# Fused layer chain: a front with split loads and another embedding layout, and one grid operation placed ahead of each division of the attention

## The chip, the cores and the metric

The kernel runs on one core of a Trainium2 chip. Its time is the device time of one execution in microseconds, and the median of several executions is compared. Beside it there is one execution recorded by the hardware profiler, from which all durations below are read. Engines are named as in the profile: PE is TensorE (PEld its weight loads), DVE is VectorE, ACT is ScalarE, POOL is GpSimd, SP is SyncE, which here only issues transfers. A "q" behind an engine's name means its queue of issued transfers.

## The reference, cut to what matters

Eight samples of 512 x 512 float32 pass through four layers. The first two are touched by the change.

```python
# layer 0: one explicit time step of a grid equation, per sample f[b] (512 x 512)
Af, Bf = A_grid[None] * f[:, None], B_grid[None] * f[:, None]
df = -(grad(Af[:,0],1) + grad(Af[:,1],2)) \
     + 0.5 * (grad2(Bf[:,0],1) + grad2(Bf[:,1],2)
              + grad(grad(Bf[:,2],2),1) + grad(grad(Bf[:,2],1),2))
x = maximum(f + df * dt[:, None, None], 0)      # one-sided formulas at all four borders

# layer 1: attention block, 16 heads of 32, an additive bias per head, a mask per sample
emb = silu(sin_emb(timestep)) @ W_ada + b_ada    # (8, 1024)
scale, shift = split(emb)
x = layernorm(x) * (1 + scale) + shift
q, k, v = x @ Wq + bq, x @ Wk + bk, x @ Wv + bv
p = softmax(where(mask, -inf, q @ k.T / sqrt(32) + bias))
x = x + (p @ v) @ Wo + bo
x = x + gelu2(layernorm2(x) @ W1 + b1) @ W2 + b2
# layer 2: an MLP with the weights of one of 8 experts per sample (expert_idx), then a layernorm
# layer 3: a low-rank response scaled by a gate and by sigmoid(safety)
```

## The kernel before, in words

A sample is held as 128 partitions of 4 rows of 512 columns (`P`, `R`, `D`). There are three stages.

**The front, `grid_stage`.** It computes layer 0 for sample 0, whole. SP loads six planes of 1 MiB in this order: `b1`, `a1`, `b0`, `a0` (planes of `B_grid` and `A_grid`), `f` (sample 0) and `b2`. Then SP loads the two halves of `W_ada` (`wada`), the small rows `bqk`, `bvc`, `bo` (`load_rows`), and the four matrices `Wq`, `Wk`, `Wv`, `Wo` (`load_w`). ACT's queue carries a few small transfers. DVE makes the combined coefficient planes `ca`, `cb`, `cc`, `ce`, `cg`, multiplies each by `f`, and PE adds the shifted products into four PSUM tiles (`add`, through shifted identities `zi`). First and last rows of all eight samples are computed apart, on 64 partitions (`fe`, `ec`, up to `xe`), from "edge rows" that POOL's queue loads; a small POOL operation, `gate_e`, holds those loads until `b1` is there. A second gate, `gate_c`, lets go POOL's stores of the six coefficient planes to DRAM (`coef_q` ... `coef_b`, 1 MiB each), which samples 1 to 7 read back later. POOL's queue then stores the edge rows' results (`xed`), behind those planes. `embed`, `embed_turn` and `embed_out` compute the embedding: PE makes it with samples on partitions (two results of 8 x 512), ACT copies it, PE turns it, DVE adds `b_ada` in eight operations, into `sc1` and `shift`. Eight transfers put the edge rows of sample 0 into `x`. DVE then forms small constants for the borders, `gab` and `gte` ("ghosts"), the last part of them from `hg`, four tiny matmuls. Last, DVE and POOL normalise `x`.

The tiles of the next stage lie in memory that the front gives up, so the first transfer of the attention (`mu`, the mask) waits until the front's last readers and transfers are done, those of `xed` among them; the transposed `x1` tiles do so too.

**The attention, `attention_stage`.** 128 units (sample `b`, group of four heads `c`, row `r`), in an order written out by hand and kept by `pin`. In the loop over `i` the masks are added to the bias tiles of unit `i+1` (POOL, `add_mask`), the softmax of unit `i` runs (DVE, then ACT), the probabilities of unit `i-1` are turned (`turned`: PE into `tr`, two buffers, then copies `pt` by DVE and ACT in turn), and the products with v of unit `i-2` are formed (`values`). Every fourth unit `divide` ends a group: PE turns the reciprocal sums (`rb`), ACT copies them (`rbs`), DVE multiplies (`ct`). Behind that comes `inverse` (a reciprocal `rs` on DVE and a copy on ACT), then loads, and then `grid_step(i, grid_sums)`: DVE's share of layer 0 for the samples 1 to 7, spread over 16 units per sample by the table `GRID`. A letter of the table is one DVE operation over 128 x 1024 elements (`grid_op`), `n` is a normalisation on ACT, `s` its statistics. `grid_gate` is a small POOL operation that holds `add_mask` until the last such operation of the unit before has ended. `x1_in` turns the normalised sample (PE, `xtr`) and evicts it with scale and shift: groups 0 and 2 by ACT, 1 and 3 by DVE.

```python
            if pair and two[2] == R - 1:
                divide(two[0], two[1])
            if old:
                inverse(*old)
            ...
            grid_step(i, grid_sums)
            grid_step(i, grid_loads)
            if i + 1 < n:
                scores(*units[i + 1])
```

Once, in unit 2, `add_bv` runs: DVE spreads `bvc` into `bvr`, PE multiplies it by `Wo` (`pb`), and DVE adds that to `bo`.

**The rest, `mlp_stage`.** Both MLPs and the gated response, in passes of 256 rows.

## Time and profile before

| | us |
|---|---|
| median of 3 runs (lowest, highest) | 2859.53 (2859.52, 2860.22) |
| the profiled execution, its own time | 2864.53 |
| the profiled execution, its span | 2862.8 |
| granted TensorE clock, mean over the span | 0.986 |
| busy: PE, DVE, ACT, POOL | 2738.6, 1945.2, 1002.7, 1495.7 |
| first softmax operation of DVE starts at | 86.04 |
| last `ct` of the attention starts at | 1164.03 |
| moved by DMA over the span | 405.60 MB |

The profiled execution took 5.0 us longer than the median of the runs. A row of a timeline reads: start, duration, engine, line of the kernel, operation, result<-sources, shape, count, and in brackets how long the engine was idle before it and what released it. A row of stretches reads: the stretch and its length, busy time of PE, PEld, DVE, ACT and POOL with their instructions in brackets, granted clock, share of the DMA engines, GB/s.

### The profile page before, as it was taken

Reading aid. Unit: us, or ns where it says so; the run is one execution under the profiler, and the core shown is the slowest. Engines: PE = TensorE matmul, PEld = TensorE weight load, DVE = VectorE, ACT = ScalarE, POOL = GpSimd, SP = SyncE. Lnnn points to the kernel's source line nnn. Section 1 sums busy time; section 2 is a strip of 40 time slices with the busy share of each in tenths; the row PEclk is TensorE's granted clock in tenths of the full one; section 3 lists DMA queues with packets and bytes.
Section 4 is the critical chain, followed back from the end, with each engine's and each line's share of the span. In section 5 each row is a group of like instructions: output and inputs, shape, how many; then the busy total and the mean of one; then the engine's idle time right before and its main releaser. Section 6 shows DMA issues by size and latency. Waiting matters only on the chain.

```text
span 2862.8 us, 39706 instructions
## 1 busy us (share of the span) xinstructions
PE 2738.6 (96%) x14606; PEld 2008.5 (70%) x14606; DVE 1945.2 (68%) x3606; ACT 1002.7 (35%) x2133; POOL 1495.7 (52%) x1062
## 2 busy tenths in 40 slices
PE   5889999999999999999999999999999999999997
PEld 2455545454545555688888888887888888888885
DVE  7788888888888766576566656664456555656554
ACT  1366666666666666212111211211121121121221
POOL 2345455555555655366465555654545545545632
PEclk9999999999999999999999999999999999999998
DMA  8655656565666555433532444253133133143120
GB/s 306 210 192 178 218 170 230 167 229 171 224 203 207 162 159 184 165 100 81 154 122 61 127 138 123 49 166 112 59 110 126 52 141 125 49 144 111 41 74 30
DMA packets 190352, 405.60 MB, mean 142 GB/s; under 512 B 24321, under 2 KB 28993, under 8 KB 183631
## 3 DMA queue, kind: packets, MB, share of 16 engines
q1 hardware_dynamic: 185170, 391.94, 41.0%
q0 software_dynamic: 3680, 11.07, 3.1%
q8 instruction: 116, 1.90, 0.3%
q14 instruction: 78, 0.63, 0.1%
q10 hardware_dynamic: 1308, 0.07, 0.0%
HBM read 367.32 MB, written 31.50 MB: 139 GB/s over the span
## 4 chain that ended last, share of the span: by engine, by line
PE 79%; DVE 14%; ACT 4%; DMA 2%; issue 1%; POOL 0%; SPq 0%; ACTq 0%; DVEq 0%; POOLq 0%
PE u L1129 27%; PE y L1129 24%; PE tr L547 6%; PE ctx L544 4%; PE s L544 4%; PE o L544 3%; PE pv L544 3%; PE pq L544 2%; DVE x L664 2%; DVE bt L968 2%; ACT bt L973 2%; DVE pt L993 2%; PE pk L544 2%; DVE tb L1135 1%; DVE act L1135 1%
## 5 line engine op out<-in xcount | busy, mean ns | idle before, releaser
L1129 PE MATMUL y<-wo,act 128*128 128x256 f32 x2560 | 578.9, 381 | 0.0
L945 POOL TENSOR_TENSOR bt<-bt,mk 128x1024 f32<-128x1024 f32 x256 | 541.8, 2138 | 58.8 <-DMA bt<-in_bias 42.6
L1129 PEld LDWEIGHTS y<-wo,act 128*128 128x128 f32 x2560 | 479.4, 190 | 82.2 <-issue 20.5
L973 ACT ACTIVATE bt<-bt,mn 128x512 f32<-128x512 f32 x512 | 365.5, 715 | 137.0 <-DVE mn L968 136.7
L547 PEld LDWEIGHTS tr<-ident,bt 128*128 128x128 f32 x2048 | 229.1, 142 | 189.7 <-issue 118.6
L1129 PE MATMUL u<-bt,wi 128*128 128x256 f32 x1440 | 332.4, 381 | 0.0
L968 DVE CUSTOM_DVE_ANT_0 bt<-s,bt 128x512 f32<-128x512 f32 x512 | 330.5, 683 | 0.0
L547 PE MATMUL tr<-ident,bt 128*128 128x128 f32 x2048 | 282.7, 280 | 38.8 <-DVE pt L993 27.7
L1135 DVE TENSOR_TENSOR act<-u,u 128x512 f32<-128x512 f32 x256 | 173.4, 687 | 212.8 <-PE u L1129 138.0
L1129 PEld LDWEIGHTS u<-bt,wi 128*128 128x128 f32 x1440 | 274.6, 191 | 37.6
L993 DVE COPY pt<-tr 128x512 f32<-128x512 f32 x256 | 175.9, 687 | 100.4 <-PE tr L547 99.7
L1129 PE MATMUL u<-tb,ws 128*128 128x256 f32 x1024 | 242.4, 380 | 0.0
L1129 PE MATMUL y<-t,s 128*128 128x256 f32 x1024 | 234.1, 380 | 0.0
L1129 PEld LDWEIGHTS u<-tb,ws 128*128 128x128 f32 x1024 | 195.1, 191 | 26.7
L995 ACT COPY pt<-tr 128x512 f32<-128x512 f32 x256 | 148.2, 579 | 183.9 <-PE tr L547 181.5
L1138 POOL TENSOR_TENSOR t<-wo,t 128x512 f32<-128x512 f32 x64 | 104.5, 1648 | 198.2 <-PE y L1129 198.2
L1129 PEld LDWEIGHTS y<-t,s 128*128 128x128 f32 x1024 | 190.6, 190 | 23.8
L1135 DVE TENSOR_TENSOR x<-y,x 128x512 f32<-128x512 f32 x96 | 64.5, 686 | 183.2 <-PE y L1129 129.2
L1441 ACT ACTIVATE act<-act,bi 128x512 f32<-128x512 f32 x128 | 83.9, 712 | 292.3 <-DVE act L1135 292.2
L1441 ACT ACTIVATE act<-act,b 128x512 f32<-128x512 f32 x128 | 82.9, 712 | 292.4 <-DVE act L1135 292.4
L1135 DVE TENSOR_TENSOR u<-u,u 128x512 f32<-128x512 f32 x192 | 131.3, 684 | 59.5 <-PE u L1129 59.5
L544 PE MATMUL s<-kt,qt 32*128 32x512 f32 x1024 | 166.9, 644 | 2.1 <-DVE mn L968 1.1
(315 smaller groups left out, 4283.2 us busy)
## 6 DMA issues: line engine op xcount, KB each, us to landing
bt<-in_bias SPq DMA_DIRECT2D x256, 512.0 KB
wo<-in_W SPq DMA_DIRECT2D x32, 1024.0 KB
wi<-in_Wi SPq DMA_DIRECT2D x32, 1024.0 KB
wo<-in_Wo_e SPq DMA_DIRECT2D x32, 1024.0 KB
wi<-in_W SPq DMA_DIRECT2D x28, 1024.0 KB
gq<-coef_q SPq DMA_DIRECT2D x21, 512.0 KB
x1d<-x SPq DMA_DIRECT2D x8, 1024.0 KB
x<-x1d SPq DMA_DIRECT2D x8, 1024.0 KB
```

Source lines behind the costliest of these rows:

```text
L544: pin(nc.tensor.matmul(out, lhsT=lhsT, rhs=rhs, start=start, stop=stop))
L547: pin(nc.tensor.transpose(out, src, ident))
L664: pin(nc.vector.tensor_tensor(out, x, y, op))
L945: nc.gpsimd.tensor_tensor(bt, bt, mask[b, r][:, None, :].to_broadcast([P, 2, S]), ALU.add)
L968: nc.vector.tensor_tensor_reduce(bt[:, i, :], ss[h], bt[:, i, :], -1.0, 3.0e38, ALU.add, ALU.min, mn)
L973: nc.scalar.activation(bt[:, i, :], bt[:, i, :], AF.Exp, bias=mn, scale=-1.0, accum_out=sums[b, c, r][:, h : h + 1],)
L993: pin(nc.vector.tensor_copy(pt[:, :, r % 2, :], tr))
L995: pin(nc.scalar.copy(pt[:, :, r % 2, :], tr))
L1129: pin(nc.tensor.matmul(out, lhsT=lhsT, rhs=rhs, start=start, stop=stop))
L1135: pin(nc.vector.tensor_tensor(out, x, y, op))
L1138: pin(nc.gpsimd.tensor_tensor(out, x, y, op))
L1441: nc.scalar.activation(acts[g][:, k, :], acts[g][:, k, :], func, bias=bi[:, j : j + 1])
```

## The change

In words, front first:

- `b1` and `a1` are loaded in halves of two rows each, in turn, and `ca` and `cb` are formed half by half. The loads of `eidx` and `sigs` go from SP's queue to ACT's.
- `gate_e` reads `f` where it read `b1`: the edge rows are let go behind `f`. Their blocks come in another order, so that the results reach `x` by two transfers on each of SP's and ACT's queues, where it were four.
- `load_w` stands ahead of `load_rows`.
- The embedding is computed with features on partitions: 32 small matmuls with `wada` as the stationary operand, and one addition on DVE (`ada`, whose parts are `sc1` and `shift`); the 1 of `1 + scale` is added to `bada` beforehand. That addition stands behind the normalisation.
- The ghosts `gab` and `gte` are formed by POOL, behind the stores of the coefficient planes and ahead of `xed`. For that, `hg` is multiplied earlier and ACT copies it into `hgs`.
- At the start of the attention the loads of sample 1 (`gf`, `gq`) stand ahead of the first bias tiles. `bvr` is formed by ACT before the first unit.
- `x1_in` evicts groups 0 and 2 by DVE, 1 and 3 by ACT.
- In the units with a division, one operation of `GRID` (ahead of the bar) runs ahead of `divide`, the others where they were.

```diff
-    sc1 = const.tile([P, KC, NB], F32, name="sc1")
-    shift = const.tile([P, KC, NB], F32, name="shift")
+    ada = const.tile([P, 2 * KC, NB], F32, name="ada")
+    sc1, shift = ada[:, 0:KC, :], ada[:, KC : 2 * KC, :]
...
+    nc.scalar.dma_start(sigs, a["safety"][None, :].to_broadcast([P, NB]))
+    nc.scalar.dma_start(eidx, a["eidx"][None, :])
+    nc.vector.tensor_scalar(bada[:, 0:KC], bada[:, 0:KC], 1.0, None, ALU.add)
...
     def embed(ps):
+        pe = ps.tile([P, 2 * KC, NB], F32, name="pe")
         for m in range(2 * KC):
             o = (m % KC) * P
+            for k in range(KC):
+                tc.keep_in_program_order(
+                    nc.tensor.matmul(
+                        pe[:, m, :], lhsT=wada[m // KC][:, k, o : o + P], rhs=sc[:, k, :],
+                        start=k == 0, stop=k == KC - 1,
+                    )
+                )
         return pe
     def embed_out(pe):
+        tc.keep_in_program_order(
+            nc.vector.tensor_tensor(
+                ada, pe, bada[:, :, None].to_broadcast([P, 2 * KC, NB]), ALU.add
+            )
+        )
...
-        blocks = (0, 1, 3, 2)
+        blocks = (0, 2, 3, 1)
...
-            rows_in(b1, a["B"][1])
-            rows_in(a1, a["A"][1])
+            halves = slice(0, 2), slice(2, 4)
+            for h in halves:
+                rows_in(b1, a["B"][1], h)
+                rows_in(a1, a["A"][1], h)
...
             load_wada()
+            load_w()
             load_rows()
-            load_w()
...
-            pin(nc.gpsimd.tensor_tensor(gate, b1[:, 0, 0:1], b1[:, 0, 0:1], ALU.add))
+            pin(nc.gpsimd.tensor_tensor(gate, f[:, 0, 0:1], f[:, 0, 0:1], ALU.add))
...
-            tt(ca, b1, a1, ALU.add)
-            tt(cb, b1, a1, ALU.subtract)
+            for h in halves:
+                tt(ca[:, h, :], b1[:, h, :], a1[:, h, :], ALU.add)
+                tt(cb[:, h, :], b1[:, h, :], a1[:, h, :], ALU.subtract)
...
         add(lambda r: c[:, r, :])
+        hg = ps.tile([P, 2, 2, 3], F32, name="hg")
+        for i in range(2):
+            for k, (r, turn) in enumerate(((R - 1, 0), (0, 2))):
+                mm(
+                    hg[:, k, i, :], zi[:, 0, turn : turn + P],
+                    b2[:, r, 509 * i : 509 * i + 3], True, True,
+                )
+        hgs = small.tile([P, 2, 2, 3], F32, name="hgs", tag="hgs", bufs=1)
+        pin(nc.scalar.copy(hgs, hg))
...
+                pin(
+                    nc.gpsimd.tensor_tensor(
+                        tab if k else gab[:, :, i, :], c[:, :, o : o + 4], w, ALU.mult
+                    )
+                )
+            pin(nc.gpsimd.tensor_tensor(gab[:, :, i, :], gab[:, :, i, :], tab, ALU.add))
...
+                    pin(nc.gpsimd.tensor_scalar_mul(dst, src, w[k]))
         t = wp.tile([P, R, D], F32, name="t")
...
-        for i, k in enumerate(blocks):
-            c = slice(W * k, W * k + W)
-            pin(nc.sync.dma_start(x[0:1, 0, c], xe[n * i : n * i + 1, :]))
-            o = n * i + NB
-            pin(nc.scalar.dma_start(x[P - 1 : P, R - 1, c], xe[o : o + 1, :]))
+        for o, u, c in ((0, 3 * n, 0), (n, n, 2 * W)):
+            for side, q_ in ((0, nc.sync), (1, nc.scalar)):
+                p, r = side * (P - 1), side * (R - 1)
+                e0 = o + side * NB
+                pin(
+                    q_.dma_start(
+                        x[p : p + 1, r, c : c + 2 * W].rearrange("o (b w) -> o b w", w=W),
+                        xe[e0 : e0 + u + 1 : u, :],
+                    )
+                )
...
         stats(2)
-        embed_out(pe)
...
-                tt(tab if k else gab[:, :, i, :], c[:, :, o : o + 4], w, ALU.mult)
-            tt(gab[:, :, i, :], gab[:, :, i, :], tab, ALU.add)
...
-                    pin(nc.vector.tensor_scalar(dst, src, w[k], None, ALU.mult))
         stats(0)
...
+        embed_out(pe)
...
-            if c % 2 == 0:
+            if c % 2:
                 pin(nc.scalar.activation(tv, trv, AF.Identity, bias=h, scale=g))
...
         GRID = {
-            0: "q0 q1", 1: "e0", 2: "w0 c0 hh", 3: "C0", 4: "+0 -0", 5: "g0", 6: "G0 a0",
-            7: "A0 b0 B0", 8: "x0 q2", 9: "e1 w1 c1", 10: "C1 +1", 11: "-1 g1", 12: "G1 s0",
-            13: "n0 a1 A1 b1", 14: "B1 x1", 15: "s1", 16: "n1",
+            0: "q0 q1", 1: "e0 |", 2: "w0 c0 hh", 3: "C0", 4: "+0 -0", 5: "g0 |", 6: "G0 a0",
+            7: "A0 b0 B0", 8: "x0 q2", 9: "e1 | w1 c1", 10: "C1 +1", 11: "-1 g1", 12: "G1 s0",
+            13: "a1 | n0 A1 b1", 14: "B1 x1", 15: "s1", 16: "n1",
         }
...
         mask_in(0, 0)
+        grid_loads(1, -2)
         load_bias(*units[0])
-        grid_loads(1, -2)
         grid_loads(1, -1)
...
+        pin(nc.scalar.copy(bvr, bvc[:, :, None].to_broadcast([P, KC, P])))
...
-            if pair and two[2] == R - 1:
+            split = pair and two[2] == R - 1
+            if split:
+                grid_step(i, lambda n, j: grid_sums(n, j, late=False))
                 divide(two[0], two[1])
...
-            grid_step(i, grid_sums)
+            grid_step(i, lambda n, j: grid_sums(n, j, early=not split))
```

More of the change, by code (lines that the diff above doesn't have):

```diff
@@ L53, in fused_kernel @@
     nc.gpsimd.memset(phalf, 0.5)
-    sc1 = const.tile([P, KC, NB], F32, name="sc1")
-    shift = const.tile([P, KC, NB], F32, name="shift")
+    ada = const.tile([P, 2 * KC, NB], F32, name="ada")
+    sc1, shift = ada[:, 0:KC, :], ada[:, KC : 2 * KC, :]
     eidx = const.tile([1, NB], I32, name="eidx")
-    nc.sync.dma_start(eidx, a["eidx"][None, :])
     sigs = const.tile([P, NB], F32, name="sigs")
-    nc.sync.dma_start(sigs, a["safety"][None, :].to_broadcast([P, NB]))
-    nc.scalar.activation(sigs, sigs, AF.Sigmoid)
     def x_home(b):
@@ L138, in fused_kernel @@
     nc.scalar.activation(sc, sc, AF.Silu)
+    nc.scalar.activation(sigs, sigs, AF.Sigmoid)
     def embed(ps):
-        keep = tc.keep_in_program_order
-        out = []
-        for h in range(2):
-            pr = ps.tile([NB, D], F32, name=f"pe_{h}")
+        pe = ps.tile([P, 2 * KC, NB], F32, name="pe")
+        for m in range(2 * KC):
+            o = (m % KC) * P
             for k in range(KC):
-                keep(
+                tc.keep_in_program_order(
                     nc.tensor.matmul(
-                        pr, lhsT=sc[:, k, :], rhs=wada[h][:, k, :], start=k == 0, stop=k == KC - 1
-                    )
-                )
-            out.append(pr)
-        return out
-    def embed_turn(ps, rows, out):
-        for h in range(2):
-            tc.keep_in_program_order(nc.scalar.copy(rows[:, h, :], out[h]))
-        pe = ps.tile([P, 2 * KC, NB], F32, name="pe_t")
-        for m in range(2 * KC):
-            o = (m % KC) * P
-            tc.keep_in_program_order(
-                nc.tensor.transpose(pe[:, m, :], rows[:, m // KC, o : o + P], ident[0:NB, 0:NB])
-            )
+                        pe[:, m, :], lhsT=wada[m // KC][:, k, o : o + P], rhs=sc[:, k, :],
+                        start=k == 0, stop=k == KC - 1,
+                    )
+                )
         return pe
     def embed_out(pe):
-        for m in range(KC):
-            for t, o, one in ((sc1, m, 1.0), (shift, KC + m, 0.0)):
-                tc.keep_in_program_order(
-                    nc.vector.tensor_scalar(
-                        t[:, m, :], pe[:, o, :], bada[:, o : o + 1], one, ALU.add, ALU.add
-                    )
-                )
+        tc.keep_in_program_order(
[3 more added lines that the diff above has]
+        )
     dram = ctx.enter_context(tc.tile_pool(name="x1_dram", bufs=1, space=bass.MemoryType.DRAM))
@@ L194, in fused_kernel @@
         tc, a, const, small, dram, xt[0], mhalf, ident, load_wada, load_w, load_rows, embed,
-        embed_turn, embed_out,
+        embed_out,
     )
@@ L229, in grid_stage @@
     tc, a, const, small, dram, x, mhalf, ident, load_wada, load_w, load_rows, embed,
-    embed_turn, embed_out,
+    embed_out,
 ):
@@ L284, in grid_stage, with rows_in @@
         dte = gp.tile([N, 1], F32, name="dte")
-        def rows_in(t, src):
-            nc.sync.dma_start(t, src.rearrange("(p r) j -> p r j", r=R))
+        def rows_in(t, src, r=slice(0, R)):
+            nc.sync.dma_start(t[:, r, :], src.rearrange("(p r) j -> p r j", r=R)[:, r, :])
         with tc.tile_pool(name="raw", bufs=1) as rp:
@@ L393, in grid_stage @@
                 pin(nc.gpsimd.dma_start(coefs[m][S + 1 : S + 2, :], w[P - 1 : P, R - 1, :]))
+        gab = const.tile([P, R, 2, 4], F32, name="gab")
+        tab = small.tile([P, R, 4], F32, name="tab", tag="tab", bufs=1)
+        for i, (u, v, o) in enumerate(((ca, cb, 0), (cb, ca, 508))):
+            for k, c in enumerate((u, v)):
+                w = gw[:, None, 8 * i + 4 * k : 8 * i + 4 * k + 4].to_broadcast([P, R, 4])
+                pin(
[4 more added lines that the diff above has]
+            pin(nc.gpsimd.tensor_tensor(gab[:, :, i, :], gab[:, :, i, :], tab, ALU.add))
+        gte = const.tile([P, R + 2, 2, 3], F32, name="gte")
+        for i, (o, w) in enumerate(((0, (-3.0, 3.0, -1.0)), (509, (1.0, -3.0, 3.0)))):
+            for k in range(3):
+                for dst, src in (
+                    (gte[:, 1 : R + 1, i, k : k + 1], b2[:, :, o + k : o + k + 1]),
+                    (gte[:, 0 : R + 2 : R + 1, i, k : k + 1], hgs[:, :, i, k : k + 1]),
+                ):
+                    pin(nc.gpsimd.tensor_scalar_mul(dst, src, w[k]))
         t = wp.tile([P, R, D], F32, name="t")
@@ L397, in grid_stage @@
         add(lambda r: t[:, r, :], 1, last=True)
-        hg = ps.tile([P, 2, 2, 3], F32, name="hg")
-        for i in range(2):
-            for k, (r, turn) in enumerate(((R - 1, 0), (0, 2))):
-                mm(
-                    hg[:, k, i, :], zi[:, 0, turn : turn + P],
-                    b2[:, r, 509 * i : 509 * i + 3], True, True,
-                )
         s2 = gp.tile([N, 2], F32, name="s2")
@@ L468, in grid_stage @@
             pin(nc.gpsimd.dma_start(xed[:, W * k : W * k + W], xe[n * i : n * i + n, :]))
-        emb = embed(ps)
+        pe = embed(ps)
         pin(nc.vector.tensor_scalar(dth, dth, 0.5, None, ALU.mult))
@@ L475, in grid_stage @@
             pin(nc.scalar.activation(x[:, r, :], x[:, r, :], AF.Relu))
-        for i, k in enumerate(blocks):
-            c = slice(W * k, W * k + W)
-            pin(nc.sync.dma_start(x[0:1, 0, c], xe[n * i : n * i + 1, :]))
-            o = n * i + NB
-            pin(nc.scalar.dma_start(x[P - 1 : P, R - 1, c], xe[o : o + 1, :]))
-        rows = wp.tile([NB, 2, D], F32, name="emb_rows")
-        pe = embed_turn(ps, rows, emb)
+        for o, u, c in ((0, 3 * n, 0), (n, n, 2 * W)):
[8 more added lines that the diff above has]
+                )
         def stats(r):
@@ L488, in grid_stage @@
         stats(2)
-        embed_out(pe)
-        gab = const.tile([P, R, 2, 4], F32, name="gab")
-        tab = small.tile([P, R, 4], F32, name="tab", tag="tab", bufs=1)
-        for i, (u, v, o) in enumerate(((ca, cb, 0), (cb, ca, 508))):
-            for k, c in enumerate((u, v)):
-                w = gw[:, None, 8 * i + 4 * k : 8 * i + 4 * k + 4].to_broadcast([P, R, 4])
-                tt(tab if k else gab[:, :, i, :], c[:, :, o : o + 4], w, ALU.mult)
-            tt(gab[:, :, i, :], gab[:, :, i, :], tab, ALU.add)
-        gte = const.tile([P, R + 2, 2, 3], F32, name="gte")
-        for i, (o, w) in enumerate(((0, (-3.0, 3.0, -1.0)), (509, (1.0, -3.0, 3.0)))):
-            for k in range(3):
-                for dst, src in (
-                    (gte[:, 1 : R + 1, i, k : k + 1], b2[:, :, o + k : o + k + 1]),
-                    (gte[:, 0 : R + 2 : R + 1, i, k : k + 1], hg[:, :, i, k : k + 1]),
-                ):
-                    pin(nc.vector.tensor_scalar(dst, src, w[k], None, ALU.mult))
         stats(0)
@@ L550, in attention_stage @@
         bqk, bvc, bo = rows
+        bvr = io.tile([P, KC, P], F32, name="bvr", tag="v0", bufs=2)
         def add_bv():
-            bvr = io.tile([P, KC, P], F32, name="bvr", tag="v0", bufs=2)
-            pin(nc.vector.tensor_copy(bvr, bvc[:, :, None].to_broadcast([P, KC, P])))
             pb = ps.tile([P, D], F32, name="pb", tag="m")
@@ L797, in attention_stage, with grid_sums @@
         GRID = {
[3 rows of a table removed]
-        }
-        def grid_sums(n, j):
-            for op in GRID.get(j, "").split():
[3 rows of a table added]
+        }
+        def grid_sums(n, j, late=True, early=True):
+            ops = GRID.get(j, "")
+            if "|" in ops and not (late and early):
+                ops = ops.split("|")[late]
+            elif not late:
+                ops = ""
+            for op in ops.replace("|", "").split():
                 if op == "hh":
```

## The prediction

> **What bounds the kernel now.** The page's chain of the work that ended last comes first: by engine it gives PE 79%, DVE 14%. In order of time PE alone carries it from 1177.99 us on, in `mlp_stage`, of which the change touches nothing. So two stretches are left: the attention (86 to 1178 us), which the waits and a timeline explain, and the front (0 to 86 us), for which the stretches, the DMA share and SP's waits are read.

> In the attention a batch of samples 2 to 7 lasts 132.4 to 135.6 us from one division to the next of its kind (387.57 to 520.01 and so on). PE's waits between 250 and 1060 us, some six such batches:

> ```profile
> PE tr L547 <- DVE pt L993: 23.7, 23, 1.9
> PE xtr L547 <- ACT x L587: 6.9, 6, 1.2
> PE tr L547 <- ACT pt L995: 4.2, 6, 0.7
> PE rb L547 <- ACT x L587: 2.6, 6, 0.4
> ```

> Columns: total, times, longest. The sum is 37.4 us, 6.0 a batch; otherwise PE runs through. All of it lies beside the divisions. The timeline of one (fourth group, where `e1 w1 c1` follow):

> ```profile
> 386.97 0.57 ACT L1024 COPY rbs<-rb 128x512 f32<-128x512 f32 x1
> ...
> 387.57 0.69 DVE L1027 TENSOR_TENSOR ct<-ctx,rbs 128x512 f32<-128x512 f32 x1 [2.02 <-ACT rbs L1024]
> ...
> 391.64 0.68 DVE L993 COPY pt<-tr 128x512 f32<-128x512 f32 x1
> ...
> 392.38 0.66 PE L547 MATMUL tr<-ident,bt 128*128 128x128 f32 x4 [1.94 <-DVE pt L993]
> ```

> DVE stands 2.02 us for `rbs`, then works `ct`, `rs` and three grid operations at 1.14 us each (388.26, 389.37, 390.51), and PE waits 1.94 us for the copy behind them. The first grid operation needs nothing of the division.

> In the front, look at the share of the DMA engines (last but one column):

> ```profile
> 44.00:46.00 2.00, 2.00 (x6) 0.81 (x5) 1.90 (x6) 0.00 (x0) 0.00 (x0) 1.00 1.04 419
> ...
> 58.00:60.00 2.00, 2.00 (x7) 0.41 (x6) 0.00 (x0) 0.61 (x2) 0.00 (x0) 1.00 0.60 221
> 60.00:62.00 2.00, 0.68 (x8) 0.50 (x7) 0.96 (x8) 0.54 (x1) 0.00 (x0) 1.00 0.01 2
> ```

> SP's waits up to 110 us:

> ```profile
> SPq L287 <- DMA bada<-in_b_ada: 5.8, 1, 5.8
> ...
> SPq L565 <- DMA xed<-xe: 3.8, 1, 3.8
> ...
> SPq L565 <- DVE gte L505: 1.7, 1, 1.7
> ```

> The DMA engines are full (share 1.0) from 6 to 58 us, whoever computes what. Then they stand for 5 us: `mu`, issued at 63.96, waits 3.8 us for the landing of `xed` and 1.7 us for the ghosts. One more idle stretch is in unit 2, where DVE, PE and DVE follow each other:

> ```profile
> 114.05 0.96 DVE L554 COPY bvr<-bvc 128x512 f32<-128x512 f32 x1
> ...
> 115.15 5.19 PE L544 MATMUL pb<-Wo,bvr 128*128 128x512 f32 x8 [4.81 <-ACT bt L973]
> ...
> 120.37 0.69 DVE L558 TENSOR_TENSOR bo<-pb,bo 128x512 f32<-128x512 f32 x1 [5.37 <-PE pb L544]
> ```

> **Part 1, one operation ahead of the division.** Nothing is added; an operation of 1.14 us moves into DVE's wait.
> - Fourth group (`e1`, samples 2 to 7, 6 times): wait 2.02 > 1.14, so `ct` isn't delayed, `pt` comes 1.14 us sooner, and PE's 1.94 falls to 0.8. 6 x 1.14 = 6.8 us.
> - First group (`a1`, samples 1 to 7): wait 2.02 to 2.09. PE waits 0.70 us for ACT's `pt` (behind `n0`, which stays) and then 1.24 us for DVE's; the second falls to 0.1. 7 x 1.14 = 8.0 us.
> - Third group (`g0`, 6 times): wait 1.13, PE waits only 0.24: 6 x 0.24 = 1.4 us. The rest is slack of DVE.
> - Second group (`e0`): wait 0.89; PE doesn't wait for DVE there. 0.

> The moved operation needs its coefficients some 2.6 us sooner. They are issued at least two units (16 us) ahead, and among DVE's waits between 100 and 1200 us no grid product waits for a DMA: cost 0.

> [...] Row: `gq<-gq,gq` at 329.79 took 1.95 us instead of 1.22, while POOL's second mask addition ran until 330.66. [...] An addition lasts 2.14 us; blocked for a whole one, an operation ahead of `ct` gains nothing (1.14 - 2.14 + the 0.8 left of the wait), and part 1 would be 0. By the rows POOL is done at 385.26 and DVE free at 385.54, at the other divisions POOL is done 1 to 4 us earlier. I take the rows: 16.2 us.

> **Part 2, `x1_in` swapped.** PE waits 1.15 us for ACT to empty the first `xtr` (ACT is still at four exponentials and `kt` until 320.6), then 0.43 us before `rb`; DVE meanwhile stands 1.12 us for the second. With DVE on the first, `xtr` 2 starts at about 320.65 instead of 321.41, `rb` at 322.1 instead of 322.94, `rbs` likewise. 0.85 us, 7 times: 6.0 us.

> **Part 3, `bvr` by ACT.** The chain was `bvr` 1.0, `pb` 5.2 (PE idle 4.8 us, granted clock 0.68 in 115 to 120), `bo`. With `bvr` there, PE does `pb` from 110.4 and ends near 114; DVE reaches `bo` at 114.05 instead of 120.37. 6.3 us; at least the 4.8 of PE. ACT's copy (about 0.6 us) lies before `kt`, which waits 7.4 us for PE.

> **Part 4, the front.**
> - Loads: `b1` is issued 0.84 us sooner. But by the instruction order of the changed kernel the second half of `b1` waits for the landing of the first, and that of `a1` for `bada`. [...] By the trace (first load issued 1.59, bytes flow from about 4.2 at 420 GB/s) 1 MiB of first halves flows to about 6.0; the second half of `b1`, issued at about 6.2 on a landing, flows from about 7.3 (`mu`, issued at 63.96, had its bytes flowing an us later): a gap of 1.3 against 0.84 won, so 0.5 us later. On DVE the new operation on `bada` stands ahead of the angle chain and `ca`, and waits for `bada` (landed about 8.3 before): `ca` starts near 9 to 10 instead of 10.75.
> - Edge rows behind `f`: rates fell from 400 to 240-290 GB/s between 14 and 24 us, when they ran beside the planes. Without them `a0` comes near 17 instead of 18.86, `f` near 20 instead of 24.0, and `e` starts near 21.5: 2.5 us sooner, and PE's sums with it. The rows then land by my estimate near 34 (1024 pieces of some 516 bytes, 64 per DMA engine, now between the 2 KB packets of the matrices and no longer the 8 KB packets of the planes), needed near 39.
> - Embedding: PE's 16 matmuls of 7.0 us become 64 with their own weights; `hg`, the nearest row, takes 0.95 us for 8, so 7.6. ACT's two copies, eight turns and DVE's 5.7 us of waiting go. The normalisation no longer stands behind it. The ghosts' 18 operations (0.1 us pitch on DVE) go to POOL at about 0.2 each (its gates take 0.19), 3.6 us, ahead of `xed`, which queues behind `coef_b` anyway.
> - What decides is the DMA: the same 19.8 MB, full from 6 to 58 us, then `xed` lands near 62. So `x` is ready before its memory is: `mu` can go at about 62.3 instead of 63.96, only the ghosts' 1.7 us.
> - Then the new order: `gf` and `gq` (2.5 MB) no longer stand behind 1 MB of bias. `gq` lands about 9 us after `mu` instead of 13; `coef_e`, behind both, 13 us after, near 75.4. DVE's chain q0 q1 e0 w0 c0 then puts the first softmax at about 80 instead of 86.04. 6.0 us. Bounds: 0 (lost to the gap and late edge rows, e.g. another 3 us) and 12 (if the freed DMA time brings `xed` 6 us sooner).

> **Sum.** 16.2 + 6.0 + 6.3 + 6.0 = 34.5 us. Against the profiled execution: 2864.5 - 34.5 = 2830. That execution was 5.0 above the median of the runs, 2859.5, so the median would be 2825. A difference under 0.2% (5.7 us) can't be told from none.

> **The rivals.**
> - Front gives nothing, the rest holds (chance 0.2): edge rows land after DVE wants them at 39 us, DVE and PE stand, the small loads behind the matrices come late. For it: the full DMA. Against: slack of some 3 us between `x` and the landing of `xed`. -28.5: 2831.
> - PE's stalls at the divisions change their releaser (0.15): ACT's `pt` and exponentials follow DVE closely (ACT waits 115 us for DVE's minima), and half of parts 1 and 2 comes back as waits for ACT. For it: the 0.70 us already there. 34.5 - 11 = 23.5: 2836.
> - Edge rows give more (0.13): `xed` lands near 56. -40 to -46: 2816.
> - Slower (0.04): POOL's second mask addition ends after the early operation wants to start, at every division. It decides from the point where POOL ends 2.2 us later than now (387.5 in the timeline above): then each division gains nothing, and each further us is lost 25 times. To eat the other 18.3 us and 5.7 more, 1 us per division, POOL must end 3.2 us late. Its gate opens 4.4 us before, so bias tiles 3 us late would do it (POOL waited 28.8 us for them in 14 places). 2866.
> - Not as said (0.03): the moved operations do run ahead by the instruction order, but the time falls to where nothing waits, within 0.2%: 2857.

> The forecast itself has 0.45. It reaches from 2819 to 2831. With the first two and part of the third the range is 2814 to 2838. Faster 0.93, same 0.03, slower 0.04.

> **What would show it.** Right: DVE's wait for `rbs` falls from 52.0 us to about 20; PE's for `pt` from 23.7 to under 10; `rb` no longer waits for ACT; batches of 129 to 132 us; `pb` starts before DVE's `bo` is due; first softmax near 80. Wrong in the front: a DVE wait for `ec` or `fe`, or `mu` later than 63. Wrong in the attention: grid operations of 2 us ahead of `ct`, PE waiting for ACT's `pt`, or batches still of 132 to 135.

## The result, and the profile after

The changed kernel takes 2829.9 us (median of 4 executions, 2828.87 to 2831.33), the kernel before beside it 2859.88 us (2859.52 to 2865.43). The ratio is 0.9891, with a 95% interval of 0.9874 to 0.9908: 31 us less, between 26 and 36. The forecast was 2825, with a range of 2814 to 2838. The profiled execution of the changed kernel took 2828.87 us, with a span of 2826.4: 36.4 us less than the span of before.

Where the 36.4 us went can be read at three landmarks, the start of the same operation in both profiles:

| landmark, start in us | before | after | gained so far |
|---|---|---|---|
| first softmax operation of DVE | 86.04 | 88.28 | -2.2 |
| first `ct` | 150.09 | 146.00 | 4.1 |
| last `ct` of the attention | 1164.03 | 1127.48 | 36.6 |
| end of the span | 2862.8 | 2826.4 | 36.4 |

So the front lost 2.2 us, the stretch with `pb` gained 6.3, the attention 32.5, and the rest nothing. The forecast had said 6.0, 6.3 and 22.2.

**The attention.** PE's waits between 250 and 1060 us (total, times, longest):

```profile
PE tr L546 <- DVE pt L998: 5.6, 10, 0.8
PE tr L546 <- ACT pt L1000: 4.2, 6, 0.7
PE xtr L546 <- DVE x L588: 2.8, 6, 0.5
PE rb L546 <- DVE x L588: 1.3, 6, 0.2
```

The first was 23.7 us with a longest of 1.9; ACT's 4.2 us are the same as before, so the releaser did not change. The timeline of a fourth-group division:

```profile
371.99 1.22 DVE L663 TENSOR_TENSOR x<-x,gf 128x1024 f32<-128x1024 f32 x1
373.49 0.57 ACT L1029 COPY rbs<-rb 128x512 f32<-128x512 f32 x1
...
374.09 0.69 DVE L1032 TENSOR_TENSOR ct<-ctx,rbs 128x512 f32<-128x512 f32 x1 [0.88 <-ACT rbs L1029]
...
377.03 0.68 DVE L998 COPY pt<-tr 128x512 f32<-128x512 f32 x1
...
377.77 0.66 PE L546 MATMUL tr<-ident,bt 128*128 128x128 f32 x4 [0.81 <-DVE pt L998]
```

One grid operation now starts at 371.99, ahead of `ct`; DVE's wait for `rbs` is 0.88 us instead of 2.02, and PE's behind it 0.81 instead of 1.94.

**The unit with `pb`.** The rows of `pb` and `bo` (before, they started at 115.15 and 120.37, each behind a wait of about 5 us):

```profile
112.81 3.60 PE L543 MATMUL pb<-Wo,bvr 128*128 128x512 f32 x8
...
116.45 0.69 DVE L557 TENSOR_TENSOR bo<-pb,bo 128x512 f32<-128x512 f32 x1
```

PE waits for nothing ahead of `pb`, and DVE for nothing ahead of `bo`. `pb` itself takes 3.60 us instead of 5.19: the granted clock between 115 and 120 us is 1.00 where it was 0.68.

**The front.** The stretches (columns as in the prediction: busy time of PE, PEld, DVE, ACT, POOL, then granted clock, share of the DMA engines, GB/s). First the start of the loads, before:

```profile
6.00:8.00 2.00, 0.00 (x0) 0.00 (x0) 1.23 (x8) 1.18 (x4) 0.00 (x0) 1.00 1.03 420
8.00:10.00 2.00, 0.00 (x0) 0.00 (x0) 0.00 (x0) 1.46 (x2) 1.93 (x4) 1.00 1.08 381
10.00:12.00 2.00, 0.00 (x0) 0.00 (x0) 1.25 (x1) 0.00 (x0) 2.00 (x5) 1.00 1.01 355
```

And after, with the end of the transfers:

```profile
6.00:8.00 2.00, 0.00 (x0) 0.00 (x0) 0.90 (x6) 0.30 (x1) 0.00 (x0) 1.00 0.73 163
8.00:10.00 2.00, 0.00 (x0) 0.00 (x0) 1.06 (x7) 1.97 (x3) 0.00 (x0) 1.00 0.50 150
10.00:12.00 2.00, 0.00 (x0) 0.00 (x0) 1.21 (x3) 1.38 (x4) 0.00 (x0) 1.00 0.84 269
...
60.00:62.00 2.00, 2.00 (x11) 2.00 (x11) 0.00 (x0) 0.00 (x0) 0.00 (x0) 0.50 0.95 368
62.00:64.00 2.00, 1.22 (x6) 1.12 (x6) 0.45 (x1) 0.00 (x0) 0.00 (x0) 0.50 0.37 116
```

There is a hole in the loads between 6 and 12 us (150 to 269 GB/s where it was 355 to 420), and the engines are busy until about 62.7 us where they had been idle from 60 on. SP's waits up to 110 us name what it waited for:

```profile
SPq L274 <- DMA b<-in_B: 4.2, 1, 4.2
...
SPq L564 <- DMA xed<-xe: 2.1, 1, 2.1
...
SPq L274 <- DMA bada<-in_b_ada: 1.3, 1, 1.3
```

The second half of `b1` waited 4.2 us for the first, as the order of the instructions had said. `mu`, issued at 64.59 instead of 63.96, still waits for `xed`; the wait for the ghosts is gone, as predicted, but nothing is won by it.

### The profile page after: what moved, and what is told of

It is laid out like the page before. It is cut to its first block, busy times and chain, and to the rows that moved or that the text cites. A ratio compares the mean times of both kernels' runs of the same rounds, so it can differ in the third digit from the quotient of the medians.

```text
span 2826.4 us, 39775 instructions
## 1 busy us (share of the span) xinstructions
PE 2731.6 (97%) x14646; PEld 2013.2 (71%) x14646; DVE 1942.6 (69%) x3583; ACT 1003.3 (35%) x2133; POOL 1502.6 (53%) x1080
## 4 chain that ended last, share of the span: by engine, by line
PE 81%; DVE 13%; ACT 2%; issue 1%; POOL 0%; DVEq 0%; POOLq 0%; ACTq 0%
PE u L1137 27%; PE y L1137 24%; PE tr L546 6%; PE s L543 4%; PE ctx L543 4%; PE o L543 3%; PE pv L543 3%; PE pq L543 3%; PE pk L543 2%; DVE bt L973 2%; DVE tb L1143 2%; DVE x L663 1%; DVE pt L998 1%; ACT bt L978 1%; DVE act L1143 1%
## 5 line engine op out<-in xcount | busy, mean ns | idle before, releaser
L973 DVE CUSTOM_DVE_ANT_0 bt<-s,bt 128x512 f32<-128x512 f32 x512 | 330.4, 683 | 0.0
L1143 DVE TENSOR_TENSOR x<-y,x 128x512 f32<-128x512 f32 x96 | 64.6, 686 | 182.5 <-PE y L1137 128.5
```

The source lines that it names most:

```text
L973: nc.vector.tensor_tensor_reduce(bt[:, i, :], ss[h], bt[:, i, :], -1.0, 3.0e38, ALU.add, ALU.min, mn)
L1143: pin(nc.vector.tensor_tensor(out, x, y, op))
```

## The experiments

### Each part alone

Four kernels, each the kernel before with one part of the change. The kernel before took 2861.79 us beside them (35 executions, 2856.38 to 2867.66). By their ratios the four parts make 37 us together; the whole change makes 31 by its first runs and 35 by its later ones (below), with intervals of some 5 us either way, so no loss or gain of the parts against one another is shown.

**Part 1 alone** (the bar in `GRID`, and the early call; the table and the change of `grid_sums` are left out):

```diff
...
+            split = pair and two[2] == R - 1
+            if split:
+                grid_step(i, lambda n, j: grid_sums(n, j, late=False))
                 divide(two[0], two[1])
...
-            grid_step(i, grid_sums)
+            grid_step(i, lambda n, j: grid_sums(n, j, early=not split))
```

> The kernel before with part 1 alone: one grid operation ahead of each division, all else as before. The prediction's sum: 16.2 us less, about 2843. Rival (clock): the waits of PE for DVE's copy behind a division (1.94 us in the profile of before) now and then drop the granted clock to 0.5 for 3 to 4 us; six such places (near 258, 292, 558, 660, 694 and 828 us) cost some 8 us in the profiled execution of before. By it no stretch between 250 and 1060 us falls below a clock of 0.97 here, all batches are alike to 0.1 us at about 129.8, and the profiled execution gains 16 and up to 8 us more, more than the median does. Against it: batches still scatter by 1 to 3 us. Third view (releaser changes): half of it returns as waits for ACT, 8 us less, about 2851.

Measured: 2836.41 us, ratio 0.9917 (0.9903 to 0.9931): 24 us less, between 20 and 28, not 16.2. The predicted part is there. In an undisturbed batch of the profiles, the time from the `ct` of the named group to the next `ct` is (us):

| | from second | from third | from fourth | from first | batch |
|---|---|---|---|---|---|
| before | 31.97 | 31.36 | 33.05 | 36.06 | 132.44 |
| part 1 alone | 31.81 | 30.94 | 31.92 | 34.95 | 129.62 |
| parts 1 and 2 (the changed kernel) | 31.97 | 30.93 | 31.92 | 34.15 | 128.97 |

Part 1 gains 2.82 us a batch, 16.9 in six, and 1.6 in the first. The rest is the clock: in this profile no stretch between 170 and 1060 us is below a clock of 0.97, and the batches are alike to 0.15 us. Two divisions of the same kind in the kernel before (columns as above; the borders of these stretches are explained below):

```profile
254.74:258.15 3.41, 1.47 (x8) 0.74 (x7) 3.41 (x5) 0.00 (x0) 0.74 (x2) 1.00 0.47 154
258.15:261.57 3.42, 3.42 (x8) 1.50 (x6) 2.75 (x9) 3.07 (x8) 3.42 (x2) 0.50 0.39 99
...
387.86:391.27 3.41, 2.59 (x12) 1.34 (x10) 3.41 (x5) 0.78 (x2) 0.00 (x0) 1.00 0.64 207
391.27:394.69 3.42, 2.31 (x8) 1.07 (x9) 3.42 (x10) 1.72 (x5) 2.82 (x3) 1.00 0.17 54
394.69:398.10 3.41, 3.41 (x41) 1.64 (x40) 3.38 (x8) 1.88 (x6) 1.55 (x1) 1.00 0.37 133
```

At both PE waited 1.94 us for DVE's copy. The first wait lies whole in one stretch (PE is busy for 1.47 of 3.41 us), and in the next stretch the granted clock is 0.5. The second wait is divided between two stretches (0.82 and 1.11 us), and the clock stays at 1. Of the 12 such places between 250 and 1060 us (six fourth groups, six first groups) the clock fell at 6. The interval is longer by about 1.0 us each time: 34.03 instead of 33.05, 37.12 instead of 36.06. With part 1, PE's longest wait for that copy is 0.8 us, and the clock fell at 0 of 12 places:

```profile
PE xtr L547 <- ACT x L587: 6.9, 6, 1.2
PE tr L547 <- DVE pt L998: 6.4, 11, 0.8
```

So the clock theory holds for the profiled executions, and the third view (waits for ACT) is out.

The traces also show which places lose the clock. In each of the 14 traces (all runs of this document) the granted clock changes only on a grid of 3.413 us (to within 0.005 us), and the grid lies differently against the kernel's start in each execution (its first border comes 2.94 and 1.31 us after the start in the two profiles of the changed kernel). The stretches above are cut on it. The four profiles that keep the long waits (before, and parts 2, 3 and 4 alone) have 25 stretches of the grid between 250 and 1060 us in which PE stands for 1.91 us or more; 24 of them are followed by one stretch at 0.5. Behind stretches with 1.84 us or less the clock did not fall in any of the 14 traces there. So a wait of 1.94 us cost about 1.0 us more than itself when it fell whole into one stretch of the grid, and which waits did so changed from profile to profile (6 of 12 places before, 8 of 12 with part 2 alone).

If a wait of PE cost its own length and no more, part 1 would come to the 18.5 us of the batches (16.9 and 1.6). By the rows such a wait cost 1.0 us more where it fell whole into one stretch of the grid, six times in the profiled execution of before: some 6 us.

**Part 2 alone.**

```diff
-            if c % 2 == 0:
+            if c % 2:
                 pin(nc.scalar.activation(tv, trv, AF.Identity, bias=h, scale=g))
```

> The kernel before with part 2 alone: x1_in evicts groups 0 and 2 by DVE, 1 and 3 by ACT. The prediction's sum: 0.85 us at each of 7 first-group divisions, 6.0 us less, about 2853.5. Rival: without part 1 DVE has other work ahead of its copy for PE, so that an earlier rbs only lengthens DVE's lead and less than 2 us come out. By the clock theory this one keeps the 1.94 us waits of PE, and so stretches at a clock of 0.5 to 0.7 are still seen between 250 and 1060 us, with batches that scatter by 1 to 3 us.

Measured: 2858.13 us, ratio 0.9989 (0.9983 to 0.9995): 3.1 us less, between 1.4 and 4.9. PE's waits:

```profile
PE tr L547 <- DVE pt L993: 21.8, 22, 1.9
PE tr L547 <- ACT pt L995: 4.2, 6, 0.7
PE xtr L547 <- DVE x L589: 2.8, 6, 0.5
```

`xtr` waits 0.5 us instead of 1.2 and `rb` 0.2 instead of 0.4, as worked out. But the long waits for `pt` remain, and in this profile the clock fell at 8 of the 12 places, at all six of the first groups; their interval is 36.2 to 36.5 us, against 37.1 before where the clock fell and 36.06 where it did not. On top of part 1 the swap is worth 129.62 - 128.97 = 0.65 us a batch. By itself the part gives half of the 6.0, which lies outside the interval; the rival's "less than 2 us" is still inside it. The third expectation, clock drops that stay, is met in the profile; that they make up the missing 3 us in the other executions is not shown.

**Part 3 alone.**

```diff
+        bvr = io.tile([P, KC, P], F32, name="bvr", tag="v0", bufs=2)
+
         def add_bv():
-            bvr = io.tile([P, KC, P], F32, name="bvr", tag="v0", bufs=2)
-            pin(nc.vector.tensor_copy(bvr, bvc[:, :, None].to_broadcast([P, KC, P])))
...
+        pin(nc.scalar.copy(bvr, bvc[:, :, None].to_broadcast([P, KC, P])))
         add_mask(*units[0])
```

> The kernel before with part 3 alone: bvr formed by ACT ahead of the first unit. The prediction's sum: 6.3 us less (at least 4.8), about 2853; bo ends ahead of 115 instead of 121 us. Rival: the memory of bvr (the tag of v0) or ACT's copy delays the first kt or v, and 2 us of it are lost again. Clock theory: PE's wait of 4.8 us goes, and with it the granted clock of 0.89 between 115 and 130 us becomes 1.0.

Measured: 2852.04 us, ratio 0.9965 (0.9952 to 0.9979): 10 us less, between 6 and 14. The timeline:

```profile
109.30 3.60 PE L544 MATMUL pb<-Wo,bvr 128*128 128x512 f32 x8
...
113.16 0.68 DVE L558 TENSOR_TENSOR bo<-pb,bo 128x512 f32<-128x512 f32 x1
```

`bo` starts at 113.16; in the profiles of parts 1 and 2 alone, which have the front of before too, it starts at 120.21 and 120.40. That is 7.1 us. The first `ct` follows by the same amount (142.69 against 149.75 and 149.96), so nothing of it is given back, and the rival is out. The granted clock between 115 and 130 us is 1.00 instead of 0.89, as the clock theory said. The interval of the time holds the 7.1 us as well as the 6.3 predicted.

**Part 4 alone**: the changed kernel with parts 1 to 3 taken back.

```diff
+            pin(nc.vector.tensor_copy(bvr, bvc[:, :, None].to_broadcast([P, KC, P])))
...
-            if c % 2:
+            if c % 2 == 0:
...
-            0: "q0 q1", 1: "e0 |", 2: "w0 c0 hh", 3: "C0", 4: "+0 -0", 5: "g0 |", 6: "G0 a0",
+            0: "q0 q1", 1: "e0", 2: "w0 c0 hh", 3: "C0", 4: "+0 -0", 5: "g0", 6: "G0 a0",
...
-        pin(nc.scalar.copy(bvr, bvc[:, :, None].to_broadcast([P, KC, P])))
...
-            if split:
-                grid_step(i, lambda n, j: grid_sums(n, j, late=False))
+            if pair and two[2] == R - 1:
                 divide(two[0], two[1])
...
```

> The kernel before with part 4 alone: the whole front as changed (halves, edge rows behind f, embedding with features on partitions, ghosts on POOL, first loads of sample 1 ahead of the bias), the attention as before. The prediction's sum: 6.0 us less, first softmax near 80, about 2853.5. Theory from the trace after: the front gains nothing, it costs 2.2 us: first softmax near 88.3 instead of 86.0, e near 24.1, edge rows late (a DVE wait for ec near 43), mu near 64.6, and DVE's first operations of sample 1 slowed by POOL's mask addition (4.3 us for q0 q1, 3.1 us for e0); about 2861.7.

Measured: 2861.12 us, ratio 0.9999 (0.9991 to 1.0007). The front is worth nothing, to within some 2.5 us; 6.0 us less (0.9979) is excluded. First softmax at 87.41, where the profiles with the front of before have 84.59 to 86.04.

### One step of the front taken back

Four kernels, one profiled execution each (2826.8, 2826.5, 2829.1 and 2829.3 us in the order below), so they are read by landmarks and not by times. The changed kernel's own two profiles (the second is shown below) differ by 1.0 us in the first softmax: what is less than that is not told apart here.

```diff
-            for h in halves:
-                rows_in(b1, a["B"][1], h)
-                rows_in(a1, a["A"][1], h)
+            rows_in(b1, a["B"][1])
+            rows_in(a1, a["A"][1])
```

> The changed kernel with b1 and a1 loaded whole (ca and cb still half by half). Theory (the halves open a hole in the loads: SP waits 4.2 us for the first half of b1, and the DMA engines move 150 to 270 GB/s between 6 and 12 us where it was 355 to 420): here the planes flow at 350 GB/s and more from 6 us on, e starts near 21.5 to 22.5 instead of 24.1, the edge rows come 2 us sooner, mu is issued near 62.5 instead of 64.6, first softmax near 86. Rival: the order of the planes and the small loads makes e what it is: e at 24 and all behind it as in the changed kernel.

The theory was wrong in its reason. `e` starts at 22.98 and the first softmax at 85.72, about the figures expected, but the hole in the loads is still there:

```profile
4.00:6.00 2.00, 0.00 (x0) 0.00 (x0) 0.00 (x0) 0.00 (x0) 0.30 (x1) 1.00 0.82 271
6.00:8.00 2.00, 0.00 (x0) 0.00 (x0) 1.03 (x7) 0.94 (x1) 0.00 (x0) 1.00 0.38 54
8.00:10.00 2.00, 0.00 (x0) 0.00 (x0) 0.93 (x6) 1.96 (x4) 0.00 (x0) 1.00 0.75 274
```

SP's waits up to 36 us say why:

```profile
SPq L274 <- DMA ti<-in_tok: 5.7, 1, 5.7
```

`a1`, second on SP's queue, waited 5.7 us for the landing of `ti`, a 4 KB transfer of ACT's queue. In each of the three versions SP's loads wait for something earlier: for `bada` 5.8 us before, for the first half of `b1` 4.2 us in the changed kernel, for `ti` here. `ti` is issued at 0.74 in all three; it reached DVE at 3.37 us before, where the first plane was issued at 1.59, but at 6.00 in the changed kernel and 6.87 here, where the plane was issued at 0.75. Before, two planes (2 MiB) were under way when SP came to its wait; now it is 1 MiB. In that, by my reading, lies the hole, more than in the halves as such. That the earlier plane, and so the late `ti`, came with the move of `eidx` and `sigs` from SP's queue to ACT's is argued only; a kernel with those two put back was not run.

```diff
-            pin(nc.gpsimd.tensor_tensor(gate, f[:, 0, 0:1], f[:, 0, 0:1], ALU.add))
+            pin(nc.gpsimd.tensor_tensor(gate, b1[:, 0, 0:1], b1[:, 0, 0:1], ALU.add))
```

> The changed kernel with gate_e on b1, as before: the edge rows run beside the planes. Theory (bytes are only moved about): e later by 2 to 3 us (26 to 27), DVE no longer waits for ec near 43, the DMA engines end the front at the same time, mu within a us of 64.6, first softmax within a us of 88. Rival (the late edge rows delay the front): xe and xed a us or two sooner, mu near 63, first softmax near 86.5.

`e` at 28.18, 4 us later, and no wait for `ec`; `xe` at 54.81, 3 us later, and yet `mu` at 63.23 and the first softmax at 86.74. These two are where the rival had them, but not for its reason, since `xe` came later and not sooner; the softmax is only 0.5 us from the changed kernel's second profile. The front's end does not follow `xe`. By my reading the last of the transfers ends it: they end near 61.2 us instead of 62.7, and the edge rows filled a part of the hole (share of the DMA engines between 8 and 10 us 0.83 instead of 0.50). Something else changed with it, though:

```profile
38.34 3.45 SPq L178 DMA_DIRECT2D bo<-in_bo  x1
```

SP's issue of `bo` takes 3.45 us here and 14.11 in the changed kernel (next experiment), so SP sends the edge rows into `x` at 57.0 instead of 60.4. No run separates the two.

```diff
-            load_w()
             load_rows()
+            load_w()
```

> The changed kernel with load_rows ahead of load_w, as before. Theory (SP sits in the issue of bo, 14.1 us behind the full queue of the four matrices, and so issues the transfers of x from xe only at 60.4): here they are issued near 53 to 55, DVE's last statistics come near 57 to 59 instead of 63.55, xtr some 2 to 3 us sooner than 68.8, and mu is unchanged near 64.6, since it waits for the landing of xed. The first softmax hangs on coefficients behind mu and stays within a us of 88. Rival: this delay is what the front lost: first softmax near 85.

The block is real. In the changed kernel:

```profile
39.48 14.11 SPq L178 DMA_DIRECT2D bo<-in_bo  x1
...
60.42 1.38 SPq L492 DMA_DIRECT2D x<-xe  x2
...
63.55 0.70 DVE L499 BATCH_NORM_STATS2 ln_st<-x 128x6 f32<-128x512 f32 x1 [6.84 <-DMA x<-xe]
```

And with the rows first:

```profile
53.75 1.38 SPq L492 DMA_DIRECT2D x<-xe  x2
...
61.54 0.69 DVE L499 BATCH_NORM_STATS2 ln_st<-x 128x6 f32<-128x512 f32 x1 [4.76 <-DMA x<-xe]
```

SP is free 6.7 us sooner, but DVE's wait for these transfers of 1 KB still ends only at 61.5, 7.8 us behind SP's issue of its two and 6.4 behind ACT's (55.13). `xtr` comes 2.0 us sooner (66.78); `mu` does not (65.12). The first softmax is at 86.74, between the 88 of the theory and the 85 of the rival, and not told apart from the changed kernel's second profile (87.29).

```diff
-        grid_loads(1, -2)
         load_bias(*units[0])
+        grid_loads(1, -2)
```

> The changed kernel with the first bias tiles loaded ahead of gf and gq, as before. Theory (POOL's first mask addition, 5.9 us from 78 on, collides with DVE's q0 q1 and e0 and stretches them from 2.6 and 1.2 us to 4.3 and 3.1): here the addition runs near 73 to 77 while DVE waits, q0 q1 take 2.6 us and e0 1.2, and the first softmax comes near 86 instead of 88.3 though gq lands later. Rival (bytes decide): gq and coef_e land 3 us later, q0 starts near 81, first softmax at 88 or later.

The theory holds. In the changed kernel (timeline, DVE and POOL):

```profile
77.06 0.75 DVE L617 TENSOR_SCALAR qt<-pq,bqk 128x512 f32<-128x512 f32 x1 [4.63 <-PE pq L543]
77.72 4.28 DVE L663 TENSOR_TENSOR gq<-gq,gf 128x1024 f32<-128x1024 f32 x2
78.05 5.94 POOL L950 TENSOR_TENSOR bt<-bt,mk 128x1024 f32<-128x1024 f32 x2 [11.44 <-DMA bt<-in_bias]
81.93 3.14 DVE L663 TENSOR_TENSOR x<-x,gf 128x1024 f32<-128x1024 f32 x1
```

With the bias tiles first:

```profile
74.76 4.22 POOL L950 TENSOR_TENSOR bt<-bt,mk 128x1024 f32<-128x1024 f32 x2 [7.30 <-DMA gf<-in_x]
...
78.43 2.77 DVE L663 TENSOR_TENSOR gq<-gq,gf 128x1024 f32<-128x1024 f32 x2
81.12 1.21 DVE L663 TENSOR_TENSOR x<-x,gf 128x1024 f32<-128x1024 f32 x1
```

POOL's two additions take 4.22 us instead of 5.94, and DVE's three operations 4.0 instead of 7.4. First softmax 85.54, 1.8 and 2.7 us sooner than in the two profiles of the changed kernel, although `q0` starts later. The loads of sample 1, put ahead, had bought nothing: DVE comes to `q0` only behind `qt`, which waits for PE's `pq`.

### Steps put together

Four kernels beside one another, 4 executions each: the changed kernel again; the kernel before with the diffs of parts 1, 2 and 3; the changed kernel with the first, third and fourth of the four diffs above; and that with the second too. The kernel before took 2862.36 us here (7 executions).

> The changed kernel again, beside the three next ones. By its first runs 2829.9 us, about 30 below the kernel before; executions within some 2.5 us of each other, since no wait of 2 us is left at the divisions that could drop the clock. First softmax near 88, first ct near 146.

> The kernel before with parts 1, 2 and 3, its front and its order of the first loads left as before. By the prediction's sum (the front worth 6.0 us) it would take 6 us more than the changed kernel: about 2836. By the traces so far (the changed front ends 1 to 3 us later: first softmax 87.4 to 88.3, against 84.6 to 86.0 with the front of before) it takes 1 to 3 us less: about 2827, first softmax near 85.3, first ct near 143.

> The changed kernel with three of its steps taken back together: b1 and a1 whole, load_rows ahead of load_w, first bias tiles ahead of gf and gq. Edge rows behind f, the new embedding and the ghosts on POOL stay. Each of the three by itself brought the first ct 1.5 to 2.9 us forward. Theory (three separate losses, one chain): they add in part, first softmax near 83, first ct near 140.5 to 141.5, about 2825. Rival (one bound, the bytes ahead of the landing of xed): together no more than the best alone, first softmax near 85.5, first ct near 143, about 2827.

> As the one before, and gate_e on b1 again: of the changed front only the computing parts are left (embedding with features on partitions, ghosts on POOL, results of the edge rows by fewer transfers). If the late edge rows help (fewer small packets beside the planes), this one is 1 to 3 us slower than the one before: e near 24 instead of 23, first softmax near 84.5. If they only move bytes about, both are alike within a us. If the new computing parts are worth something by themselves, it is 1 to 3 us faster than the kernel with the whole front of before: about 2825.

| kernel | us (lowest, highest) | ratio to before (95%) | first softmax | first `ct` |
|---|---|---|---|---|
| the changed kernel again | 2827.74 (2827.10, 2829.39) | 0.9876 (0.9859, 0.9892) | 87.29 | 144.84 |
| parts 1 to 3, front of before | 2827.45 (2826.35, 2828.12) | 0.9874 (0.9857, 0.9890) | 84.75 | 142.43 |
| changed, three steps taken back | 2824.39 (2823.07, 2827.09) | 0.9867 (0.9850, 0.9884) | 82.76 | 140.29 |
| the same, and `gate_e` on `b1` | 2826.04 (2825.70, 2827.60) | 0.9872 (0.9856, 0.9889) | 83.51 | 141.19 |

Parts 1 to 3 alone give the whole gain: with the front of before the time is the same as that of the changed kernel (0.3 us less), not 6 us more. The version with three steps taken back has the lowest time of all, 3.4 us below the changed kernel; that is 0.12%, less than the 0.2% named in the prediction as what can be told, but the landmark stands 4.5 us earlier in the profile. Its first operations:

```profile
72.14 0.75 DVE L616 TENSOR_SCALAR qt<-pq,bqk 128x512 f32<-128x512 f32 x1 [4.51 <-PE pq L542]
75.10 1.23 DVE L662 TENSOR_TENSOR gq<-gq,gf 128x1024 f32<-128x1024 f32 x1 [2.21 <-DMA gq<-coef_q]
```

`qt` comes 4.9 and 3.9 us sooner than in the two profiles of the changed kernel, and now `q0` does wait for its coefficients. The theory of losses that add in part holds. `gate_e` on `b1` beside whole loads costs 3.7 us at `e` (26.47 against 22.81), but 0.75 at the first softmax, which is less than is told apart here, and 1.7 in the time, where the ranges of the two overlap: whether letting the edge rows go behind `f` helps is not shown. The same kernel is 1.4 us below the one with the whole front of before (2826.04 and 2827.45), again with ranges that overlap, so the computing parts of the new front are not shown to be worth anything either.

## Why the prediction was right or wrong

The total was right (34.5 us against 35.7 between the profiled executions), but not by its terms.

| term | predicted | shown in the profiles |
|---|---|---|
| part 1 | 16.2 | 18.5 (2.82 a batch, 1.6 in the first) |
| part 2 | 6.0 | 5.8 (over part 1: 0.65 a batch, 1.9 in the first, of which about 1.0 is the clock) |
| part 3 | 6.3 | 6.3 in the changed kernel, 7.1 alone |
| part 4 | 6.0 | -2.2 |
| granted clock behind PE's waits | not in the sum | 6.2 (six times 1.0) |
| one long `grs` | not in the sum | 2.1 |
| sum | 34.5 | 36.7 (the spans differ by 36.4) |

- **Part 1, right.** DVE's wait for `rbs` was to fall from 52.0 us to about 20: it is 27.0 in the changed kernel and 25.1 with part 1 alone. PE's for `pt` was to fall under 10: 5.6. The third group was undersized (0.24 a batch, measured 0.43). POOL's additions did not stand in its way, as the rows had said: all 25 early operations take 1.22 us, none is held up. (PE's waits of 37.4 us are 6.2 a batch, not the 6.0 written; nothing rests on it.)
- **Part 2, right in its mechanism**: `rb` no longer waits for ACT. In the first batch it seems worth 1.9 us, but there the clock is at 0.5 for 6.8 us in the changed kernel's first profile and for 10.2 in its second, where that interval is 1.0 us longer (37.20 instead of 36.24). Alone the part gives half; the long waits stay there.
- **Part 3, right**: PE's wait ahead of `pb` and DVE's ahead of `bo` are both gone.
- **Part 4, wrong.** Its rival, that the front gives nothing, is what happened, and both signs named against it came: a wait for `ec`, and `mu` later than 63. Three steps failed. First the loads: the gap was put at 1.3 us, from one wait; SP had three waits between 1.6 and 10.5 us, and between 6 and 12 us only 1.2 MB were moved instead of 2.3 (the three rates above, times 2 us each). So `e` starts at 24.12, not 21.5, the edge rows keep DVE waiting 1.42 us for `ec` at 43.05, where they were to be there ahead of 39, and the DMA ends at about 62.7. Second, the end of the chain: "`gq` lands 9 us after `mu`" was taken for the start of `q0`. But `qt` stands ahead of `q0` on DVE and waits for PE until 77.06, so an earlier landing could save no more than DVE's waits for coefficients behind `qt`. In the profile of before these were 1.8 us (0.33, 1.02 and 0.44, the last for `coef_c`), and there were none in that of parts 1 to 3 with the front of before:

```profile
77.50 2.56 DVE L664 TENSOR_TENSOR gq<-gq,gf 128x1024 f32<-128x1024 f32 x2 [0.33 <-DMA gq<-coef_q]
81.07 1.23 DVE L664 TENSOR_TENSOR x<-x,gf 128x1024 f32<-128x1024 f32 x1 [1.02 <-DMA x<-coef_e]
```

Third, POOL's mask addition, whose bias tile was moved back, now runs into `q0` and `e0` (3.4 us). This third step is the largest of the loss: `q0` starts at 77.72 where it was 77.50, so the hole and the late edge rows had cost at most 0.2 us by then, and the rest of the 2.2 us is lost behind it. POOL's additions had been weighed at the divisions, where they did no harm; the place where they counted was this one, and the prediction hadn't looked for POOL's next start behind the transfer that was moved.
- **Embedding**: 64 matmuls (the trace has two for each of the 32 in the code) were put at 7.6 us and took 9.85, at a granted clock of 0.5 from about 57 us on. In the changed kernel that lay beside the wait for `x` and cost nothing.
- **The clock was not in the sum, and it made up for part 4.** Six times 1.0 us, and 2.1 of one long `grs` (2.06 us at 573.34), were in the profiled execution of before and gone after (the drops because part 1 shortens the waits; the long `grs` comes and goes in profiles of both kinds). Against that stand 6.0 + 2.2 = 8.2 us of the front. That these two cancel is chance.
- **From the profiled execution to the median**: 5.0 us were taken off because the profiled execution of before was 5.0 above its median. But what lay in that excess could be just what the change removes, and the profiled execution after is not above its median (2828.87 against 2829.9). Without that step the sum gives 2830. The executions of before scatter over 11 us (35 of them), those of the versions with part 1 and part 3 together over 2 to 4; that fits clock drops that come and go with the place of the grid. But with part 1 alone it is 6.4 us, and with part 3 alone 6.9. The mean granted clock of every execution is known to 0.001: among the 35 of before, the five at 0.986 took 2862.6 to 2867.7 us and the four at 0.989 took 2856.4 to 2860.1. Among the 22 of part 2 alone and the 14 of part 4 alone no such relation is seen. That drops make the scatter of the executions without a profile is thus likely for the kernel before, and not shown in general.

What stays open: which order of the small loads would close the hole at 6 to 12 us, and what shifts POOL's additions against `grs` in one batch of some profiles and in no batch of others.

## What to carry to other kernels

A wait of PE can cost more than its length (here 1.94 us cost about 1.0 us more at 6 of 12 places of one execution), so look at the granted clock behind such waits in several places, and in more than one profile, before the sum is made, and count its loss as part of what shortening them gives. When transfers are put in another order, follow each of them to the operation that it releases and ask what that operation will then overlap, and what else its reader still has ahead of it. A total that comes out right says little about its terms: the parts run one by one showed here that the largest rewrite of the change, the front, brought nothing.

## What the runs showed of the hardware that was not expected

```profile
414.04 8.40 POOL L950 TENSOR_TENSOR bt<-bt,mk 128x1024 f32<-128x1024 f32 x4
...
420.35 2.11 DVE L781 TENSOR_SCALAR grs<-gmv 128x2 f32<-128x2 f32 x1
```

It has two elements a partition, is as short as 0.17 us elsewhere, and here ended with POOL's last addition (422.46 and 422.44). That batch was 2.1 us longer. It is no single case: in the 14 profiles an addition of POOL had 0.2 us or more to go at the start of `grs` 188 of 196 times, and each time `grs` ended within 0.05 us of the addition. It was long where it started just behind the start of one: at 420.35 here, where the last of the four began near 420.3 (8.40 us / 4 = 2.10 each, my estimate).
- Issuing 256 KB (`bo`) took SP 14.11 us behind the four matrices and 2.38 us ahead of them, and what SP had to issue next waited for it. The place in the queue is not all of it: also behind the matrices it took 8.71 us with the planes loaded whole, and 3.45 us with the edge rows let go at `b1`.
